# Edge weights in the scores of each quad, or in the one-hot matrices of each group

## The chip, the cores and the metric

One Trainium2 chip, one core. The metric is the device time of one execution in microseconds (us), as the median of several runs. The engines are named as in the profile: PE is TensorE (PEld its weight loads), DVE is VectorE, ACT is ScalarE, POOL is GpSimd, SP is SyncE.

## The reference

A graph layer over 6250 nodes (128 features, 8 heads of 16) and 206,250 edges, sorted by receiver. All is float32.

```python
w_ij = jax.nn.silu(edge_feats @ rad_W1 + rad_b1) @ rad_W2 + rad_b2
w_ij = w_ij + (jax.nn.silu(chi_scalar @ sph_W1 + sph_b1) @ sph_W2 + sph_b2)
w_ij = w_ij.reshape(-1, NUM_HEADS, HEAD_DIM)
q_i = (node_feats @ Wq).reshape(-1, NUM_HEADS, HEAD_DIM)[receivers]
k_j = (node_feats @ Wk).reshape(-1, NUM_HEADS, HEAD_DIM)[senders]
alpha = (q_i * w_ij * k_j).sum(axis=-1) / jnp.sqrt(jnp.float32(HEAD_DIM))
alpha = alpha * cutoffs[:, None]
v_j = (node_feats @ Wv)[senders].reshape(-1, NUM_HEADS, HEAD_DIM)
out = jax.ops.segment_sum(alpha[..., None] * v_j, receivers, num_segments=n_nodes) / AVG_NUM_NEIGHBORS
...
x = _layernorm(x + out)
```

`cutoffs` is the edge weight, one number for an edge. Each edge's message is its sender's `v`, scaled per head by `alpha`; messages are summed at the receiver.

## The kernel before

**Tiles.** 128 edges are a tile (one edge a partition), 4 tiles a quad (512 edges), 4 quads a group (2048 edges). There are 403 quads in 101 groups; the last group has three. Since edges are sorted by receiver, a quad's receivers lie in a window of 32 rows, and a group's in a window of 128.

**Before the loop** `k` and `v` of all nodes are computed and stored in HBM as `kv_tab` (1 KB a row), index tables are made, and `scale`, the edge weights of all tiles (128 x 1616), is multiplied by 1 / (4 x 16) (L463).

**Gathers.** For each tile GpSimd issues one indirect DMA (helper `gather`, L127), which fetches the 128 senders' rows of `kv_tab` into `kv`. It reads its list of row numbers from `src_i` in SBUF. `kv` has 16 buffers of a quad; the gathers of a quad are issued 14 quads ahead in program order (`AHEAD`), behind a mark of TensorE. In 26 of the quads, spread evenly, the fourth tile is fetched by SyncE with plain DMAs instead (`load_rows`, tile `wide`). The first 10 quads don't gather from the table; they gather rows of `x` (40 gathers into `msg`) and compute `k` and `v` themselves.

**One iteration of the loop** takes one slot of a group, quads in the order 0, 2, 1, 3. The order of each engine's work is written out by hand. Per quad:

- TensorE: first layers of both feature networks into `ph` (L472); `q` at the edges, `pq`, as a product with the transposed one-hot `hotT` (L481); second layers on edges into `pw` (L512, L517); and the sums of the group before, `po`, as products of `hot` and `msg` (L565, in `sum_quads`).
- ScalarE: the silu of `ph` into `act` (L502).
- VectorE: `kq = pq * kv` for the next quad (`multiply`, L526), then for this quad `kq = pw * kq` (L534), the reduction over 16 elements a head into `alpha` (L536), `alpha = alpha * scale` (L540), and `msg = v * alpha` (`messages`, L553).

`alpha` is a slice of the tile `side`, which lies in PSUM. So do `colp` and `rowwp`, the column and row numbers that the one-hots are compared with:

```python
aux = ctx.enter_context(tc.tile_pool(name="aux", bufs=1, space=PSUM))
side = aux.tile([P, QT * P], F32, name="side")
colp, rowwp = side[:, :P], side[:, P:P + 1]
alphas = side[:, 2 * P:2 * P + QT * HEADS].rearrange("p (t h) -> p t h", h=HEADS)
```

**Once a group**, beside the quads: `one_hots_T` (L218) makes `hotT` from `relb`, which a DMA brings, in slot 1; `statistics` (L623, L625, L626) adds `x` to the sums of an earlier group and takes its mean and variance, in slot 3, and every fourth group `normalize` follows it; `one_hots` (L223) makes the next group's `hot` in slot 3: 128 edges x 16 tiles x 32 window rows, 1.0 where the edge's receiver is that row. `hot` has 3 buffers.

**The last group** has one-hots over all 128 rows of its window (`wide_one_hots`), which ScalarE multiplies with `scale` (`weigh_wide`); its quads go through `scores` with `weighted=False` and leave L540 out.

Of the kernel before, what the change touches and what calls it, by code (L numbers as in the profile page):

```python
# [17 lines left out]
OP = mybir.AluOpType  # L18
AX = mybir.AxisListType
# [5 lines left out]
P = 128  # L25
N = 6250
D = 128
HEADS = 8
HD = D // HEADS
R = 32  # L30
E = 206250
GT = 16
QT = 4
# [9 lines left out]
W = 32  # L43
# [17 lines left out]
def gnn_kernel(ctx, tc, x, src, dst, weight, edges, rad_W1, rad_b1, rad_W2, rad_b2,  # L61
# [14 lines left out]
    nc = tc.nc  # L76
# [13 lines left out]
    scale = const.tile([P, NT], F32, name="scale")  # L90
# [32 lines left out]
    def quad_of(name, bufs, width=D):  # L123
        return ep.tile([P, QT, width], F32, name=name, bufs=bufs)
# [13 lines left out]
    feats_of, relb_of, act_of, kv_of, hot_of, hotT_of, x_of, q_of, msg_of = ({} for _ in range(9))  # L138
# [31 lines left out]
    def kv_parts(q, t):  # L170

        if q not in row_quads:
            return [(t, kv_of[q][:, t, :])]
        return [(slice(0, QT - 1), kv_of[q][:, :QT - 1, :]), (slice(QT - 1, QT), row_of[q])]
# [46 lines left out]
    def one_hots(g):  # L221
        hot_of[g] = gp.tile([P, GT, W], F32, name="hot", bufs=3)
        nc.vector.tensor_tensor(  # L223
            hot_of[g], rel[:, g * GT:(g + 1) * GT, None].to_broadcast([P, GT, W]),
            colp[:, None, :W].to_broadcast([P, GT, W]), op=OP.is_equal)

    def rows_from(table, at):

        return table.bitcast(U8).rearrange("n b -> (n b)")[ds(at, P * D * 4)].rearrange(
            "(p b) -> p b", p=P)  # L230
# [30 lines left out]
    with tc.tile_pool(name="nodes", bufs=1) as nodes, \  # L261
# [135 lines left out]
        def store_rel(a, b):  # L397
            for i, n in ((slice(a, min(b, NT // P)), P), (slice(NT // P, b), NT % P)):
                if i.start < i.stop:
                    t = slice(i.start * P, i.start * P + (i.stop - i.start) * n)  # L400
                    nc.sync.dma_start(rel_lin[t, :].rearrange("(n p) e -> p n e", p=n), relT[:n, i, :])
# [14 lines left out]
        n = len(chunks)  # L416
# [17 lines left out]
        for i, (k, n) in enumerate(work):  # L434
# [5 lines left out]
            if i >= len(chunks):  # L440
                kv_of[k[0]] = kvs
                a = (i - len(chunks)) * 5 // 4
# [18 lines left out]
        nc.vector.tensor_tensor(bsum, b2[:, 0:1], b2[:, 1:2], op=OP.add)  # L461
        store_rel(1, math.ceil(NT / P))
        nc.vector.tensor_scalar(scale, scale, SCALE, None, op0=OP.mult)  # L463


    with tc.tile_pool(name="ps", bufs=1, space=PSUM) as pp:
# [19 lines left out]
        def after(o, mark, reason="one signal of TensorE a quad"):  # L486
            tc.add_manual_dep(o.ins, mark.ins.name, WAIT, reason=reason)

        def behind(o, marks, k):

            if marks:
                after(o, marks[k], "a signal of TensorE behind the quad's own")

        def first_layers(q):

            return [hidden_of(q, i) for i in range(2)][-1]
# [12 lines left out]
        def weigh(q):  # L509

            pw = pp.tile([P, EQ], F32, name="pw", bufs=2)
            nc.tensor.matmul(pw, onesb, brow.rearrange("p t d -> p (t d)"), start=True, stop=False)  # L512
            pw = pw_of[q] = pw.rearrange("p (t d) -> p t d", d=D)
            marks = []
            for t in range(QT):
                for i in range(2):
                    o = nc.tensor.matmul(pw[:, t, :], act_of[q, i][:, t * P:(t + 1) * P], w2[:, i, :],  # L517
                                         start=False, stop=(t == QT - 1 and i == 1))
                    marks.append(o)
            return marks  # L520
# [7 lines left out]
                if mark is not None:  # L528
                    after(o, mark)

        def scores(q, t=slice(0, QT), marks=(), weighted=True):
            n = t.stop - t.start
            m = kq_of[q][:, t, :]
            nc.vector.tensor_tensor(m, pw_of[q][:, t, :], m, op=OP.mult)  # L534
            alpha = alphas[:, t, :]
            o = nc.vector.tensor_reduce(alpha, m.rearrange("p t (h e) -> p t h e", e=HD), AX.X, OP.add)  # L536
            behind(o, marks, 1)
            if not weighted:
                return alpha
            o = nc.vector.tensor_tensor(  # L540
                alpha, alpha,
                scale[:, q * QT + t.start:q * QT + t.stop, None].to_broadcast([P, n, HEADS]),
                op=OP.mult)
            behind(o, marks, 2)
            return alpha

        def messages(q, alpha, t=slice(0, QT), marks=()):

            if t.start == 0:
                msg_of[q] = quad_of("msg", XQ)  # L550
            for u, kv in kv_parts(q, t):
                n = u.stop - u.start
                o = nc.vector.tensor_tensor(  # L553
                    msg_of[q][:, u, :].rearrange("p t (h e) -> p t h e", e=HD),
                    kv[:, :, D:].rearrange("p t (h e) -> p t h e", e=HD),
                    alpha[:, u.start - t.start:u.stop - t.start, :, None].to_broadcast(
                        [P, n, HEADS, HD]), op=OP.mult)
                behind(o, marks, 3)
# [134 lines left out]
        marks = weigh(order[0])  # L693
        mark = marks[-1]
        for g in range(NG - 1):
            for slot, j in enumerate((0, 2, 1, 3)):
                q = g * NQ + j
                i = g * NQ + slot
                turned, past = None, mark
                if slot == 0 and g == CHECK + len(checks) + 1:  # L700
                    verdict()
                if slot == 0:
                    turned = turn_q(g + 1, pp.tile([P, EQ], F32, name="pq", bufs=2))
                if slot == 1 and 2 <= g:
                    turned = sum_group(g - 2)
                if slot == 2:
                    turned = make_q(g + 1, pp.tile([P, EQ], F32, name="pq", bufs=2))
                if 1 <= g:
                    for t in ((), (0, 1), (2,), (3,))[slot]:
                        mark = sum_quads(g - 1, t)  # L710
                first_layers(order[i + 2])
                mark = q_at_edges(order[i + 1])
                marks = weigh(order[i + 1])
                silus(order[i + 2], mark)
                if turned:
                    turned()
                if 1 <= g and slot == 3:
                    part_sums(g - 1)
                if i + AHEAD < len(order):
                    gathers(order[i + AHEAD], [past] * QT)  # L720
                multiply(order[i + 1], mark)
                messages(q, scores(q))
                if slot == 0:
                    if g + XL < NG:
                        load_x(g + XL, past)
                if slot == 2:
                    if g + 3 < NG:
                        load_feats(g + 3, past)
                    if g + 2 < NG:
                        load_rel(g + 2)  # L730
                if slot == 1:
                    one_hots_T(g + 1)
                    if g + 2 < NG:
                        pick(g + 2)
                    if 1 <= g:
                        place(g - 1)
                write_rows()
                load_rows(i)
                if slot == (3 if g < NG - 2 else 2):
                    if 2 <= g:  # L740
                        statistics(g - 2)
                if slot == 3:
                    if g + 1 < NG - 1:
                        one_hots(g + 1)
                    if CHECK <= g < CHECK + len(checks):
                        checks[g - CHECK]()
                if g == NG - 3 and slot in (0, 2):
                    wide_one_hots(order[slot // 2 - 3])
                if g == NG - 2 and slot == 0:
                    wide_one_hots(order[-1])  # L750
                    n = nc.values_load(general, min_val=0, max_val=1)
                    place(g)
                    place(NG - 1)
                if g == NG - 3 and slot in (1, 3):
                    weigh_wide(order[slot // 2 - 3])
                if g == NG - 2 and slot == 1:
                    weigh_wide(order[-1])
# [4 lines left out]
        marks = weigh(b)  # L762
# [4 lines left out]
        sd = roots(g - 3, g - 2)  # L767
        turned()
        part_sums(g - 1)
        messages(a, scores(a, weighted=False))  # L770
        multiply(b, mark)
        normalize(g - 3, g - 2, sd)
        write_rows()
# [3 lines left out]
        marks = weigh(c)  # L777
# [3 lines left out]
        for t in range(QT):  # L781
            sum_wide(a, t)
        nc.tensor.matmul(po_of[g], to_of[g][:, 1, :], tot_of[g - 1], start=False, stop=False)
        messages(b, scores(b, weighted=False))
        for t in range(QT):
            sum_wide(b, t)
        moments(g - 2, tot_of[g - 2], nc.gpsimd)
# [2 lines left out]
        sd = roots(g - 2, g)  # L790
        normalize(g - 2, g, sd)
        write_rows(2)
        alpha = scores(c, weighted=False)
        for h in halves:
            messages(c, alpha[:, h], h)
            for t in range(h.start, h.stop):
# [167 lines left out]
```

## Time and profile before

| what | value |
|---|---|
| runs | 2004.41 us median of 3 (2003.67 to 2005.16) |
| profiled execution | 2009.52 us |
| its span, first to last instruction | 2007.7 us |
| mean granted clock of TensorE | 0.920 |
| busy: TensorE / VectorE / ScalarE / GpSimd | 89% / 73% / 36% / 75% |

The profile is one execution. Rows of groups read: line, engine, operation, out<-in, shapes, count, then busy us and mean ns of one, then the idle time of that engine just before them and what ended it. Rows of the timeline read: start, length, engine, line, operation, and in brackets the idle time ahead with what ended it. Rows of waits read: engine and line that waited, for whom, us in total, how many times, the longest. Gathers are rows of L127 on POOL; what is seen there is the engine's own part, not the transfer.

### The profile page before, as it was taken

To read this page: it belongs to the slowest core of one execution; us is meant where nothing else is said; L and a number is where in the kernel's file an instruction comes from. 1 tells how busy PE (TensorE), PEld (TensorE's weight loads), DVE (VectorE), ACT (ScalarE), POOL (GpSimd) and SP (SyncE) were. 2 spreads that over 40 slices of the span, in tenths; PEclk is the share of its full clock that TensorE was granted. 3 is DMA by queue.
4 is the path that set the end of the run, shared out by engine and by line. 5 is a ranking of instruction groups with operands and counts; after the bars stand their busy time and mean duration, and the time that the engine had idled before them with its cause. 6 is when DMAs were issued, how large, how long until landed. Compare 5 with 4: busy or idle time off the path is not lost.

```text
span 2007.7 us, 48345 instructions
## 1 busy us (share of the span) xinstructions
PE 1795.3 (89%) x16014; PEld 1504.9 (75%) x16014; DVE 1469.9 (73%) x3075; ACT 716.0 (36%) x1437; POOL 1508.0 (75%) x1596
## 2 busy tenths in 40 slices
PE   9999899989798889898998898898988988988887
PEld 8788787778687777777787786777767777777776
DVE  6688687868687767776776777677767767767777
ACT  3244344424243233243242342333433323333334
POOL 7777777777777777777777777777777777777775
PEclk9899989989999899998889999989989888998898
DMA  8545555555555545545545445554455455455453
GB/s 313 160 141 153 149 148 154 153 141 154 154 143 153 152 143 152 154 143 150 156 143 151 140 141 154 155 155 140 140 154 154 143 150 157 138 142 157 139 154 89
DMA packets 146814, 304.33 MB, mean 152 GB/s; under 512 B 36941, under 2 KB 80061, under 8 KB 146557
## 3 DMA queue, kind: packets, MB, share of 16 engines
q0 software_dynamic: 75488, 205.36, 36.3%
q1 hardware_dynamic: 69568, 95.42, 14.7%
q8 instruction: 128, 2.10, 0.4%
q14 instruction: 130, 1.06, 0.2%
q10 hardware_dynamic: 1500, 0.40, 0.1%
HBM read 287.58 MB, written 13.46 MB: 150 GB/s over the span
## 4 chain that ended last, share of the span: by engine, by line
PE 25%; DMA 22%; DVE 18%; POOL 15%; issue 12%; SPq 4%; ACT 3%; DVEq 0%; POOLq 0%; ACTq 0%
DMA kv<-kv_tab,src_i 17%; POOL kv L127 14%; PE pw L517 11%; DVE kq L526 5%; PE pq L481 5%; PE ph L472 4%; DVE kq L534 4%; DVE side L536 4%; DMA relb<-rel_lin 3%; SPq L167 2%; PE po L565 2%; POOL msg L127 2%; DVE msg L553 2%; ACT y L645 1%; ACT L502 1%
## 5 line engine op out<-in xcount | busy, mean ns | idle before, releaser
L127 POOL DMA_INDIRECT kv<-kv_tab,src_i x1546 | 1467.5, 949 | 471.6 <-issue 393.2
L502 ACT ACTIVATE act<-ph,b 128x512 f32<-128x512 f32 x806 | 510.4, 684 | 1152.5 <-PE pq L481 1127.0
L517 PE MATMUL pw<-w,act 128*128 128x128 f32 x6448 | 900.8, 297 | 0.0
L517 PEld LDWEIGHTS pw<-w,act 128*128 128x128 f32 x6448 | 820.6, 206 | 102.7 <-issue 89.8
L481 PE MATMUL pq<-q,hotT 32*128 32x128 f32 x3224 | 497.1, 296 | 53.5 <-DVE hotT L218 33.6
L526 DVE TENSOR_TENSOR kq<-pq,kv 128x512 f32<-128x512 f32 (+1 forms) x403 | 273.9, 680 | 359.4 <-DMA kv<-kv_tab,src_i 203.2
L472 PE MATMUL ph<-feats,w 32*128 32x512 f32 x1612 | 497.7, 675 | 20.7 <-ACT act L502 19.8
L481 PEld LDWEIGHTS pq<-q,hotT 32*128 32x128 f32 x3224 | 417.6, 198 | 88.9 <-issue 46.3
L536 DVE TENSOR_REDUCE side<-kq 128x32 f32<-128x512 f32 x403 | 280.1, 695 | 13.9
L553 DVE TENSOR_TENSOR msg<-kv,side 128x512 f32<-128x512 f32 (+1 forms) x404 | 273.3, 677 | 13.8
L534 DVE TENSOR_TENSOR kq<-pw,kq 128x512 f32<-128x512 f32 x403 | 274.4, 681 | 0.0
L472 PEld LDWEIGHTS ph<-feats,w 32*128 32x128 f32 x1612 | 136.1, 192 | 106.3 <-issue 59.7
L512 PE MATMUL pw<-brow,onesb 3*128 3x512 bf16 x403 | 160.2, 397 | 14.4 <-DVE kq L534 14.2
L565 PE MATMUL po<-msg,hot 128*32 128x128 f32 x3200 | 158.5, 296 | 0.0
L218 DVE TENSOR_TENSOR hotT<-relb,side 128x512 f32<-128x512 bf16 x101 | 68.9, 682 | 92.5 <-DMA relb<-rel_lin 92.5
L606 PE MATMUL pq<-part,to 128*128 128x128 f32 x200 | 44.1, 304 | 72.1 <-DVE kq L526 53.8
L565 PEld LDWEIGHTS po<-msg,hot 128*32 128x32 f32 x3200 | 72.8, 113 | 39.6 <-issue 7.2
L606 PEld LDWEIGHTS pq<-part,to 128*128 128x128 f32 x200 | 31.6, 199 | 79.9 <-issue 54.6
L540 DVE TENSOR_TENSOR side<-side,scale 128x32 f32<-128x32 f32 x400 | 79.8, 199 | 13.7
L212 PE MATMUL pq<-wq,xT 128*128 128x128 f32 x200 | 45.9, 315 | 37.7 <-DVE kq L526 37.7
L212 PEld LDWEIGHTS pq<-wq,xT 128*128 128x128 f32 x200 | 34.7, 217 | 42.3 <-DVE kq L526 42.3
L223 DVE TENSOR_TENSOR hot<-rel,side 128x512 f32<-128x512 f32 x100 | 66.1, 661 | 0.0
(117 smaller groups left out, 852.3 us busy)
## 6 DMA issues: line engine op xcount, KB each, us to landing
wide<-kv_tab SPq DMA_DIRECT2D x3328, 1.0 KB
feats<-in_edges SPq DMA_DIRECT2D x101, 512.0 KB
kv<-kv_tab,src_i POOLq DMA_INDIRECT x1546
relb<-rel_lin SPq DMA_DIRECT2D x101, 128.0 KB
x<-in_x SPq DMA_DIRECT2D x101, 64.0 KB
out<-y SPq DMA_DIRECT2D x101, 64.0 KB
kv_tab<-kv SPq DMA_DIRECT2D x12, 512.0 KB
act<-in_x SPq DMA_DIRECT2D x12, 256.0 KB
```

What stands on the lines that cost most here:

```text
L127: return nc.gpsimd.indirect_dma_start(out=o, out_offset=None, in_=table, in_offset=bass.IndirectOffsetOnAxis(ap=index, axis=0))
L212: nc.tensor.matmul(pt[:n, :D], xT_of[g][:, :n], wq, start=True, stop=True)
L472: return nc.tensor.matmul(act_of[q, i], w1[r0:r0 + R, :], feats_of[g][r0:r0 + R, c0:c0 + EQ], start=True, stop=True)
L481: o = nc.tensor.matmul(pq_of[q][:, t, :], hotT_of[g][b, t * P:(t + 1) * P], q_of[g][b, :], start=True, stop=True)
L502: o = nc.scalar.activation(act, act_of[q, i], AF.Silu, bias=b1[:, i:i + 1])
L512: nc.tensor.matmul(pw, onesb, brow.rearrange("p t d -> p (t d)"), start=True, stop=False)
L517: o = nc.tensor.matmul(pw[:, t, :], act_of[q, i][:, t * P:(t + 1) * P], w2[:, i, :], start=False, stop=(t == QT - 1 and i == 1))
L526: o = nc.vector.tensor_tensor(kq_of[q][:, u, :], pq_of[q][:, u, :], kv[:, :, :D], op=OP.mult)
L534: nc.vector.tensor_tensor(m, pw_of[q][:, t, :], m, op=OP.mult)
L536: o = nc.vector.tensor_reduce(alpha, m.rearrange("p t (h e) -> p t h e", e=HD), AX.X, OP.add)
L553: o = nc.vector.tensor_tensor(msg_of[q][:, u, :].rearrange("p t (h e) -> p t h e", e=HD), kv[:, :, D:].rearrange("p t (h e) -> p t h e", e ...
L565: o = nc.tensor.matmul(po_of[g][j * W:(j + 1) * W, :], hot_of[g][:, j * QT + t, :], msg_of[g * NQ + j][:, t, :], start=(t == 0), stop=(t = ...
```

## The change

The multiplication of `alpha` by `scale` in each quad (L540) goes. In its place the one-hot matrix of a group is multiplied by the edge weights: `hot[p, t, w] *= scale[p, t]`, in place, one operation of 128 x 512 a group, right behind the operation that makes the one-hot matrix. The sums that use `hot` are then sums of weighted messages. For group 0 it stands ahead of the loop, behind L463, which makes `scale`. The last group is weighted by ScalarE as before, so there `scores` is the same as it was. On VectorE 400 operations go and 100 come; on the other engines the order of instructions is the same.

```diff
@@ one_hots
             hot_of[g], rel[:, g * GT:(g + 1) * GT, None].to_broadcast([P, GT, W]),
             colp[:, None, :W].to_broadcast([P, GT, W]), op=OP.is_equal)
+
+    def weigh_one_hots(g):
+        nc.vector.tensor_tensor(
+            hot_of[g], hot_of[g],
+            scale[:, g * GT:(g + 1) * GT, None].to_broadcast([P, GT, W]), op=OP.mult)
@@ before the loop
         nc.vector.tensor_scalar(scale, scale, SCALE, None, op0=OP.mult)
+        weigh_one_hots(0)
@@ scores
-        def scores(q, t=slice(0, QT), marks=(), weighted=True):
-            n = t.stop - t.start
+        def scores(q, t=slice(0, QT)):
             m = kq_of[q][:, t, :]
             nc.vector.tensor_tensor(m, pw_of[q][:, t, :], m, op=OP.mult)
             alpha = alphas[:, t, :]
-            o = nc.vector.tensor_reduce(alpha, m.rearrange("p t (h e) -> p t h e", e=HD), AX.X, OP.add)
-            behind(o, marks, 1)
-            if not weighted:
-                return alpha
-            o = nc.vector.tensor_tensor(
-                alpha, alpha,
-                scale[:, q * QT + t.start:q * QT + t.stop, None].to_broadcast([P, n, HEADS]),
-                op=OP.mult)
-            behind(o, marks, 2)
+            nc.vector.tensor_reduce(alpha, m.rearrange("p t (h e) -> p t h e", e=HD), AX.X, OP.add)
             return alpha
@@ the loop, slot 3
                     if g + 1 < NG - 1:
                         one_hots(g + 1)
+                        weigh_one_hots(g + 1)
```

The three calls `scores(a, weighted=False)`, with `b` and `c`, become `scores(a)` and so on.

More of the change, by code (lines that the diff above doesn't have):

```diff
@@ L769, in gnn_kernel @@
         part_sums(g - 1)
-        messages(a, scores(a, weighted=False))
+        messages(a, scores(a))
         multiply(b, mark)
@@ L783, in gnn_kernel @@
         nc.tensor.matmul(po_of[g], to_of[g][:, 1, :], tot_of[g - 1], start=False, stop=False)
-        messages(b, scores(b, weighted=False))
+        messages(b, scores(b))
         for t in range(QT):
@@ L792, in gnn_kernel @@
         write_rows(2)
-        alpha = scores(c, weighted=False)
+        alpha = scores(c)
         for h in halves:
```

## The prediction

> **What bounds the kernel now.** I read the page first, for the engine shares and the costliest groups.
>
> ```profile
> span 2007.7 us, 48345 instructions
> PE 1795.3 (89%) x16014; PEld 1504.9 (75%) x16014; DVE 1469.9 (73%) x3075; ACT 716.0 (36%) x1437; POOL 1508.0 (75%) x1596
> ...
> PE 25%; DMA 22%; DVE 18%; POOL 15%; issue 12%; SPq 4%; ACT 3%; DVEq 0%; POOLq 0%; ACTq 0%
> ...
> L127 POOL DMA_INDIRECT kv<-kv_tab,src_i x1546 | 1467.5, 949 | 471.6 <-issue 393.2
> ...
> L540 DVE TENSOR_TENSOR side<-side,scale 128x32 f32<-128x32 f32 x400 | 79.8, 199 | 13.7
> ...
> L223 DVE TENSOR_TENSOR hot<-rel,side 128x512 f32<-128x512 f32 x100 | 66.1, 661 | 0.0
> ```
>
> By the shares TensorE looks like the bound, and the chain that ended last is mixed. The row that decides is L127: 1546 gathers on GpSimd (POOL), 949 ns each, with idle time before them of 471.6 / 1546 = 0.305 us each. Is that gap a wait for somebody? The waits, and then GpSimd's timeline at the first gather from `kv_tab` and at the last ones, say no.
>
> ```profile
> POOL kv L127 <- issue: 393.2, 1289, 0.3
> ...
> 53.86 0.95 POOL L127 DMA_INDIRECT kv<-kv_tab,src_i  x1 [0.30 <-DVE brow L337]
> 55.11 0.94 POOL L127 DMA_INDIRECT kv<-kv_tab,src_i  x1 [0.30 <-issue]
> ...
> 1990.43 0.95 POOL L127 DMA_INDIRECT kv<-kv_tab,src_i  x1 [0.30 <-issue]
> 1991.69 0.94 POOL L127 DMA_INDIRECT kv<-kv_tab,src_i  x1 [0.30 <-issue]
> ```
>
> The longest of those gaps is 0.3 us, the same as all the others: it is the engine's own step from one gather to the next, whatever name stands as releaser. From 53.86 to 1991.69 lie 1545 steps, 1937.83 / 1545 = 1.2543 us each; 0.949 + 0.305 is 1.254. So GpSimd issues without a single pause for 1938 us, and whatever lengthens one gather moves all that follow. Whatever shortens work on another engine shortens nothing, unless it makes a gather shorter.
>
> That the others run behind this stream, and not ahead of it, shows in their own waits:
>
> ```profile
> DVE kq L526 <- DMA kv<-kv_tab,src_i: 203.2, 114, 5.3
> ...
> PE pq L606 <- DVE kq L526: 53.8, 30, 4.7
> ```
>
> VectorE waits 114 times for gathered data, and TensorE in its turn waits for VectorE's L526 to hand a `pq` bank back.
>
> **What in the trace lengthens a gather.** I went through GpSimd's timeline for gathers over 0.97 us and laid VectorE's timeline beside them. In the loop there are ten, and each has the same neighbour: L623, which adds `tot` and `x`, both in SBUF. Before the loop L367 is of that kind too (`rel` minus `qb`).
>
> ```profile
> 29.63 0.58 DVE L367 TENSOR_TENSOR rel<-rel,qb 128x400 f32<-128x400 f32 x1
> 30.05 0.98 POOL L127 DMA_INDIRECT msg<-in_x,src_x  x1 [0.30 <-issue]
> ...
> 33.84 0.95 POOL L127 DMA_INDIRECT msg<-in_x,src_x  x1 [0.30 <-issue]
> 33.89 0.59 DVE L367 TENSOR_TENSOR rel<-rel,qb 128x416 f32<-128x416 f32 x1
> ...
> 63.68 1.00 DVE L463 TENSOR_SCALAR scale<-scale 128x1616 f32<-128x1616 f32 x1
> 63.87 1.62 POOL L127 DMA_INDIRECT kv<-kv_tab,src_i  x1 [0.30 <-DVE kv L304]
> ...
> 259.98 0.28 DVE L623 TENSOR_TENSOR y<-tot,x 128x128 f32<-128x128 f32 x1
> 260.03 1.06 POOL L127 DMA_INDIRECT kv<-kv_tab,src_i  x1 [0.30 <-issue]
> ...
> 631.26 0.28 DVE L623 TENSOR_TENSOR y<-tot,x 128x128 f32<-128x128 f32 x1
> 631.36 1.01 POOL L127 DMA_INDIRECT kv<-kv_tab,src_i  x1 [0.30 <-DVE msg L553]
> ...
> 965.97 0.65 DVE L223 TENSOR_TENSOR hot<-rel,side 128x512 f32<-128x512 f32 x1
> 966.04 0.95 POOL L127 DMA_INDIRECT kv<-kv_tab,src_i  x1 [0.30 <-DMA kv<-kv_tab,src_i]
> ...
> 1061.34 0.95 POOL L127 DMA_INDIRECT kv<-kv_tab,src_i  x1 [0.30 <-issue]
> 1061.47 0.28 DVE L623 TENSOR_TENSOR y<-tot,x 128x128 f32<-128x128 f32 x1
> ```
>
> Read them in pairs. At 260 the addition ends at 260.26, 0.23 us into the gather, and the gather is 0.11 to 0.12 too long. At 631 it ends 0.18 in, and the gather is 0.06 to 0.07 too long. At 30 the subtraction ends 0.16 in: 0.03 too long. So the gather takes something 0.11 us after its start, and if such an operation is then running it waits until that ends: delay = end of the operation - start of the gather - 0.11. At 1061 and at 33.84 the operation starts after the gather's start and costs it nothing, though at 33.9 it runs 0.59 us. At 966 an operation of 0.65 us covers the gather's start, but one of its inputs is `side`, a PSUM tile: no delay. That the delay grows with the operation, the pair at 63.7 shows, another kind (one input, 1 us long): 64.68 - 63.87 - 0.11 = 0.70 by the formula, 0.67 seen. L623 is 0.28 us long, so its delays stay at a tenth; the new operation is longer.
>
> The Trainium skill's page "SBUF — State Buffer", section "SBUF: two separate sides", has the rule that VectorE and GpSimd share a port pair as an exclusive lock, and counts a VectorE operation with two SBUF inputs among the holders, against GpSimd operations that read SBUF; the pairs above agree.
>
> **The change part by part.** *Removed:* L540 in 400 quads. Its step on VectorE's queue is read between its own start and that of the messages, here in the last gather-bound place of the chain:
>
> ```profile
> 1961.63 2.71 DMA kv<-kv_tab,src_i
> ...
> 1966.57 0.21 DVE side L540
> 1966.80 0.69 DVE msg L553
> ```
>
> 0.23 us a quad, 400 x 0.23 = 92 us of VectorE time. One of L540's inputs is `side` in PSUM, so its going frees no gather. All of it lies behind the gather stream, but for one: the chain after the last data that it waits for (1964.34) runs through a single L540, worth -0.23 us at the end. The last three quads had none before.
>
> *Added:* one multiplication per group, 128x512 f32, `hot` by `scale`, both in SBUF, result in SBUF: 100 of them, of which 99 in the loop and one before it, right behind L463. Its length:
>
> ```profile
> L367 DVE TENSOR_TENSOR rel<-rel,qb 128x400 f32<-128x400 f32 x3 | 1.7, 576 | 0.1
> L367 DVE TENSOR_TENSOR rel<-rel,qb 128x416 f32<-128x416 f32 x1 | 0.6, 593 | 0.0
> L553 DVE TENSOR_TENSOR msg<-kv,side 128x512 f32<-128x512 f32 x376 | 258.2, 687 | 12.9
> ...
> L623 DVE TENSOR_TENSOR y<-tot,x 128x128 f32<-128x128 f32 x98 | 28.0, 285 | 0.0
> ```
>
> Two SBUF inputs go at (593 - 576) / 16 = 1.06 ns an element, so 593 + 96 x 1.06 = 695 ns; the 512-wide product with one PSUM input has 687. I take 0.69 us, 2.4 times an L623: 69 us in all. VectorE's time falls by 92 - 69 = 23 us, and that alone would be worth nothing, since the gather stream hides it.
>
> What costs is the port. With x the time from the multiplication's start to the next gather's, the delay is 0.69 - 0.11 - x where that is positive. If x is spread evenly over the 1.254 us of a step, the mean is 0.58 x 0.58 / 2 / 1.254 = 0.134 us, times 99 = 13.3 us. The bounds: never met 0, always met at worst 99 x 0.58 = 57 us. Whether x is even I tried on the trace: behind each one-hot operation of the loop
>
> ```profile
> L223 DVE TENSOR_TENSOR hot<-rel,side x100: 652/655/683, 45.5 to 1968.9; 128x512 f32<-128x512 f32 x100
> ```
>
> (99 of these rows, the first being before the loop) I laid an operation of 0.69 us, 0.035 us after its end as a dependent one, and 0.23 us earlier for the L540 gone in its quad, and took the delay from the recorded start of the next gather. That gives 13.9 us, 55 of the 99 being met. Without the 0.23 it is 16.8, with 0.46 (two quads without a stall between) 7.3, with 0.69 8.5. Even spread and projection agree; I take 13.0. The one before the loop I cost at nothing: it runs from about 64.7 to 65.4, and the next gather started at 65.80; if that comes to fall under it, 0.6.
>
> *Order and waits.* The multiplication waits for the one-hot just ahead of it on the same engine, and what stands behind it is the next quad's L526; in that one iteration of four VectorE carries 0.69 + 0.035 - 0.23 = 0.5 us more. TensorE's wait for `pq` can grow by that. But it trails the gathers as VectorE does, and the next three quads give 0.23 each back. The sums of the group read `hot` a whole group later. GpSimd's waits for a `kv` buffer were all met before, and VectorE reaches them no later relative to a delayed stream. No DMA and no queue is moved.
>
> Sum: 13.0 - 0.2 = +12.8 us. The profiled execution took 2009.52 us, 1.8 over its span and 5.1 over the median of the runs; it would become 2022.3, and the median 2004.41 + 12.8 = 2017.2.
>
> **The rivals.** First, no lock for this operation. Only an operation with one input, such as L463, would hold GpSimd back, and the L623 pairs would be chance. Then only the chain's end is left: 2004.41 - 0.2 = 2004.2, no change. For it: the delays seen are at most 0.12 us, on ten of 98 L623. Against it: they follow the formula to 0.03 us, and no L223 shows one. It decides if the gathers next to the multiplication stay at 0.95. The Trainium skill's same section warns of this trap for 2-port modes alone, and "VectorE: DVE Perf Modes", section "Why tensor_tensor can't do 2×_2P or 4×", keeps a tensor_tensor out of them; by those two the time would not change, and the pairs above speak against them.
>
> Second, VectorE is the bound after all. The chain gives it 18% of the span against 73% busy, so a quarter of its time lies on the chain; a quarter of 23 us is 6 us, and 2004.4 - 6 = 1998, faster. Against it stands the unbroken step of 1.254: it would need gathers that wait for VectorE, and there is none.
>
> Third, the phases lock. Where VectorE is stalled by a gather, its start is tied to the stream, and x could settle where most multiplications are met in the later two thirds: with x near 0.2 there, 66 x 0.4 + 33 x 0.134 = 31 us, 2035. The lump of 0.5 us in one quad of four, if TensorE had no slack, would go the same way (99 x 0.5 = 50 us).
>
> **How the numbers follow.** Two times within 0.2% (4 us) can't be told apart here. The forecast, 7 to 19 us more, gets 0.80; more than that 0.05; no lock 0.11; faster 0.04. The projections' ends, 7.3 and 16.8, less 0.2 and with some room for phases that shift, make 2010 to 2024; it leaves out the other cases and the fringe of mine. Slower by over 0.2% is 0.80 + 0.05 = 0.85, within it 0.11, faster 0.04.
>
> **What would show it.** Right: the median step of the gathers stays 1.25, but some 50 to 60 more gathers stand over 0.97 us, up to 1.53, each with the multiplication begun just ahead of it; their excess sums to the difference of the spans; VectorE's busy time is lower by 10 us or more and its waits for `kv` longer. Wrong: gathers all at 0.95 beside the multiplication (first rival), gaps on GpSimd over 0.3 us that end at VectorE (second), or an excess near 0.4 in nearly every group (third).

## The result and the profile after

| kernel | median | runs |
|---|---|---|
| before | 2004.85 us | 5 (2003.67 to 2005.20) |
| changed | 2015.06 us | 5 (2012.85 to 2015.29) |

The change makes the kernel slower: 10.2 us, ratio 1.0049 (95% interval 1.0035 to 1.0064). The profiled execution after took 2012.85 us, with TensorE at a granted clock of 0.914.

The page of the changed kernel, whose lines lie up to six places from where they were before (L228 is the new multiplication, L532 the former L526):

```profile
span 2011.1 us, 48012 instructions
PE 1814.8 (90%) x16014; PEld 1518.9 (76%) x16014; DVE 1460.0 (73%) x2775; ACT 716.0 (36%) x1437; POOL 1511.6 (75%) x1596
...
L127 POOL DMA_INDIRECT kv<-kv_tab,src_i x1546 | 1471.1, 952 | 471.3 <-issue 392.3
...
L228 DVE TENSOR_TENSOR hot<-hot,scale 128x512 f32<-128x512 f32 x100 | 69.4, 694 | 3.4
```

VectorE's busy time fell by 9.9 us, and the kernel got slower. The idle time ahead of the gathers is what it was (471.3 us), so GpSimd still waits for nobody. What grew is the gathers themselves. Here are the spread of their lengths (shortest, median and longest, in ns), and VectorE's wait for their data, which was 203.2 us in 114 places:

```profile
L127 POOL DMA_INDIRECT kv<-kv_tab,src_i x1546: 942/946/1709, 53.9 to 1995.1; - x194
...
DVE kq L532 <- DMA kv<-kv_tab,src_i: 252.3, 137, 5.2
```

The median gather is no longer than before (946 ns against 949); the mean is (952 against 949). In the timelines of GpSimd and VectorE, 46 gathers of the loop stand over 0.97 us, where before there were ten, and 43 of these have the multiplication just ahead. Two of the hundred places, and ahead of them a third (259.48) that is told of further down:

```profile
259.48 0.77 DVE L228 TENSOR_TENSOR hot<-hot,scale 128x512 f32<-128x512 f32 x1
259.52 0.95 POOL L127 DMA_INDIRECT kv<-kv_tab,src_i  x1 [0.30 <-issue]
...
1243.79 0.69 DVE L228 TENSOR_TENSOR hot<-hot,scale 128x512 f32<-128x512 f32 x1
1243.95 1.35 POOL L127 DMA_INDIRECT kv<-kv_tab,src_i  x1 [0.30 <-issue]
...
1422.30 0.69 DVE L228 TENSOR_TENSOR hot<-hot,scale 128x512 f32<-128x512 f32 x1
1422.35 1.47 POOL L127 DMA_INDIRECT kv<-kv_tab,src_i  x1 [0.30 <-DVE hot L223]
```

At 1422 the multiplication ends 0.64 us into the gather, and the gather is 1.47 - 0.95 = 0.52 too long; the formula of the prediction gives 0.53. At 1244 it ends 0.53 in: 0.40 seen, 0.42 by the formula. At 1401.10 a gather starts as the multiplication ends, and takes 0.95. Over all 100 places the excess sums to 8.1 us.

### The profile page after: what moved, and what is told of

Read it like the earlier page. It is cut to its first block, busy times and chain, and to the rows that moved or that the text cites. A ratio compares the mean times of both kernels' runs of the same rounds, so it can differ in the third digit from the quotient of the medians.

```text
span 2011.1 us, 48012 instructions
## 1 busy us (share of the span) xinstructions
PE 1814.8 (90%) x16014; PEld 1518.9 (76%) x16014; DVE 1460.0 (73%) x2775; ACT 716.0 (36%) x1437; POOL 1511.6 (75%) x1596
## 3 DMA queue, kind: packets, MB, share of 16 engines
q14 instruction: 128, 1.04, 0.2%
## 4 chain that ended last, share of the span: by engine, by line
PE 25%; DMA 25%; POOL 17%; DVE 16%; issue 11%; SPq 3%; ACT 2%; DVEq 0%; POOLq 0%; ACTq 0%
DMA kv<-kv_tab,src_i 22%; POOL kv L127 15%; PE pw L523 12%; DVE kq L532 5%; PE pq L487 5%; DVE kq L539 4%; PE ph L478 3%; DVE side L541 3%; DMA relb<-rel_lin 2%; PE po L562 2%; POOL msg L127 2%; SPq L167 2%; DVE msg L550 1%; PE pw L518 1%; DVE hot L223 1%
## 5 line engine op out<-in xcount | busy, mean ns | idle before, releaser
L127 POOL DMA_INDIRECT kv<-kv_tab,src_i x1546 | 1471.1, 952 | 471.3 <-issue 392.3
L523 PE MATMUL pw<-w,act 128*128 128x128 f32 x6448 | 912.1, 300 | 0.0
L523 PEld LDWEIGHTS pw<-w,act 128*128 128x128 f32 x6448 | 831.2, 209 | 104.8 <-issue 91.4
L487 PE MATMUL pq<-q,hotT 32*128 32x128 f32 x3224 | 501.3, 298 | 78.3 <-DVE kq L532 47.4
L532 DVE TENSOR_TENSOR kq<-pq,kv 128x512 f32<-128x512 f32 (+1 forms) x403 | 274.0, 680 | 396.2 <-DMA kv<-kv_tab,src_i 252.3
L228 DVE TENSOR_TENSOR hot<-hot,scale 128x512 f32<-128x512 f32 x100 | 69.4, 694 | 3.4
```

The source lines that it names most:

```text
L127: return nc.gpsimd.indirect_dma_start(out=o, out_offset=None, in_=table, in_offset=bass.IndirectOffsetOnAxis(ap=index, axis=0))
L487: o = nc.tensor.matmul(pq_of[q][:, t, :], hotT_of[g][b, t * P:(t + 1) * P], q_of[g][b, :], start=True, stop=True)
L532: o = nc.vector.tensor_tensor(kq_of[q][:, u, :], pq_of[q][:, u, :], kv[:, :, :D], op=OP.mult)
```

## The experiments

Three sets ran, each on one chip beside runs of the kernel before: the four named e, the same four again as f, and four named g. In e the chip granted TensorE a clock of 0.83, and before took 2605.43 us; in f and g before took 2007.16 and 2008.17. Theory: an operation of VectorE with two SBUF inputs holds the gather that starts under it, and it costs time because GpSimd's stream of gathers never pauses. Rival: the lump (0.7 us of extra work on VectorE, all of it in one quad of four) holds TensorE back. Ratios are to the kernel before on the same chip, with 95% intervals.

**e1 and f1: scale in PSUM.**

```diff
+    scalep = side[:, 3 * P:3 * P + GT]
...
+        nc.vector.tensor_copy(scalep, scale[:, g * GT:(g + 1) * GT])
         nc.vector.tensor_tensor(
             hot_of[g], hot_of[g],
-            scale[:, g * GT:(g + 1) * GT, None].to_broadcast([P, GT, W]), op=OP.mult)
+            scalep[:, :, None].to_broadcast([P, GT, W]), op=OP.mult)
```

> The change, but the 16 columns of scale that a group needs are first copied into PSUM (one small VectorE copy a group), and the multiplication reads hot from SBUF and scale from PSUM. Same amount of work on VectorE and a little more. Theory (two SBUF inputs hold the gathers): only the group's statistics hold a gather now, some ten gathers over 0.97 us, time as before, 2004 to 2006 us. Rival (the lump of 0.7 us on VectorE in one quad of four holds TensorE back): no better than the change, 2015 to 2018 us.

> The same kernel as in e1, again, since there TensorE was granted a clock of 0.83 and GpSimd paused for it. If GpSimd's stream is unbroken this time (before at about 2005 us): theory, 2004 to 2006 us, since e1 showed that the multiplication with scale in PSUM meets no gather; rival (lump on VectorE), 2015 to 2018 us. If TensorE bounds again: all within 0.4% of before.

f1: 2006.58 us against 2007.16, ratio 0.9998 (0.9989 to 1.0007). The whole cost of the change is gone, with the same lump on VectorE and a copy more. The page's rows of f1 for the gathers and the multiplication, and one place of its timeline:

```profile
L128 POOL DMA_INDIRECT kv<-kv_tab,src_i x1546 | 1465.2, 948 | 471.5 <-issue 388.3 <-DVE side L543 19.8 <-DVE kq L534 13.7
...
L230 DVE TENSOR_TENSOR hot<-hot,side 128x512 f32<-128x512 f32 x100 | 68.7, 687 | 3.5
...
805.78 0.69 DVE L230 TENSOR_TENSOR hot<-hot,side 128x512 f32<-128x512 f32 x1
805.98 0.94 POOL L128 DMA_INDIRECT kv<-kv_tab,src_i  x1 [0.31 <-issue]
```

The multiplication takes 687 ns, about as long as with both inputs in SBUF (694). At 805.98 it lies over the gather's start by 0.49 us; the formula would make the gather 0.38 too long, and it takes 0.94. Of the 99 in the loop 52 lie like this, by the formula worth 14.5 us together, and none lengthens a gather. The rival falls with this run: TensorE's wait in `pq` (L481) for VectorE's L526 was 19.8 us before and 47.4 after the change; the same wait is 48.8 in f1, and it costs nothing.

**e2 and f2: no weights.** `weigh_one_hots` of the change is never called; the weights are left out but in the last group.

```diff
-        weigh_one_hots(0)
...
                         one_hots(g + 1)
-                        weigh_one_hots(g + 1)
```

> The change without its multiplication: the edge weights are left out except in the last group, so 400 operations of VectorE are gone and none added (output not the reference's). Theory: VectorE lies behind the gather stream, so 92 us less work on it bring nothing but the 0.2 us at the end: 2004 to 2005 us, long gathers about ten. Rival (VectorE's time counts): a quarter of 92 us off, 1980 to 1990 us.

> The same kernel as in e2 (weights left out but in the last group), again. With an unbroken stream: theory, 2004 to 2005 us, 92 us of VectorE's work being worth nothing; rival (VectorE's time counts), 1980 to 1990 us. If TensorE bounds again: within 0.4% of before.

f2: 2006.83 us, ratio 1.0000 (0.9991 to 1.0009). Taking away the 400 small multiplications of before brings nothing that shows, though VectorE is busy for 1392.4 us against 1469.9; all of them were hidden.

**e3 and f3: the addition alone.** Before, with the change's multiplication put in (definition as in the change).

```diff
         nc.vector.tensor_scalar(scale, scale, SCALE, None, op0=OP.mult)
+        weigh_one_hots(0)
...
                         one_hots(g + 1)
+                        weigh_one_hots(g + 1)
```

> The kernel before with the multiplication of the change put in and the one per quad kept (weights twice, output not the reference's). Theory: the removal was worth nothing, so the added operation costs about what the change costs; only the phases to the gathers differ, since nothing comes 0.23 us earlier: the projection without that shift gave 16.8, even spread 13.3, so 2014 to 2022 us. Rival (VectorE's and TensorE's time counts): 92 us more than the change on VectorE, a quarter of it on the path, 2035 us or more.

> The same kernel as in e3 (multiplication added, the one per quad kept, weights twice), again. With an unbroken stream: theory, 2014 to 2022 us, the excess of its long gathers being the whole difference; rival, 2035 us or more. If TensorE bounds again: within 0.4% of before, whatever its long gathers sum to.

f3: 2021.71 us, 14.5 more than before, ratio 1.0068 (1.0054 to 1.0082). The gathers' row against that of f1:

```profile
L127 POOL DMA_INDIRECT kv<-kv_tab,src_i x1546 | 1480.6, 958 | 471.4 <-issue 395.5 <-DVE kq L540 15.0 <-DVE side L542 13.7
```

1480.6 - 1465.2 = 15.4 us of gathers, and 2021.71 - 2006.58 = 15.1 us of time (the two profiled executions differ by 15.1 as well). The lengthened gathers are the whole difference. 52 were lengthened by the multiplication here, 43 in the profile of the change.

**e4 and f4: four parts.**

```diff
-        nc.vector.tensor_tensor(
-            hot_of[g], hot_of[g],
-            scale[:, g * GT:(g + 1) * GT, None].to_broadcast([P, GT, W]), op=OP.mult)
+        for j in range(NQ):
+            t = slice(j * QT, (j + 1) * QT)
+            nc.vector.tensor_tensor(
+                hot_of[g][:, t, :], hot_of[g][:, t, :],
+                scale[:, g * GT + j * QT:g * GT + (j + 1) * QT, None].to_broadcast([P, QT, W]),
+                op=OP.mult)
```

> The change with its multiplication cut into four of 128x128, one for each quad of the group, one right behind the other. Theory, first form (a gather waits only for the one operation that it met): 0.285 us long each, delay 0.175 - x, mean 0.012 us, 396 of them, +5 us: 2009 to 2010 us. Second form (the next operation takes the port before the gather gets it): the four act as one of about 0.9 us, mean 0.25 us times 99, +25 us: 2025 to 2030 us. Rival (the lump on VectorE): 0.2 us longer than the lump of the change, 2015 to 2020 us, with no long gathers behind it.

> The same kernel as in e4 (multiplication in four parts of 128x128), again. e4 had only 4 of 100 groups with a gather lengthened beside it, so the first form is expected, a gather waits for no more than the one part that it met: with an unbroken stream 5 us, 2009 to 2010 us; the second form (the four act as one) 2025 us or more; rival (lump) 2015 to 2020 us. If TensorE bounds again: within 0.4% of before.

f4: 2009.73 us, ratio 1.0014 (1.0005 to 1.0023), 3.15 us over f1. The gathers' row of f4, and one place of the timeline, where the four stand in one row:

```profile
L127 POOL DMA_INDIRECT kv<-kv_tab,src_i x1546 | 1468.1, 950 | 471.5 <-issue 398.0 <-DVE side L544 16.2 <-DVE kq L535 13.1
...
457.55 0.90 DVE L230 TENSOR_TENSOR hot<-hot,scale 128x128 f32<-128x128 f32 x4
457.80 1.07 POOL L127 DMA_INDIRECT kv<-kv_tab,src_i  x1 [0.30 <-DVE hot L223]
```

Held by all four, the gather at 457.80 would be 458.45 - 457.80 - 0.11 = 0.54 too long; it is 0.12 too long. In the trace the parts start at 457.55, 457.76, 457.96 and 458.16, and the second ends at 458.04: the gather waited for that one, 0.24 us into it, and not for the two behind it, though the third had begun. So the first form holds; its size came out at about half of the 5 us expected. The same product of the same SBUF operands, with more busy time on VectorE (90.5 us for 69.4), costs a fifth of what it costs in one piece in f3.

**g1: a longer operation.** f1, in which the change holds no gather, and behind each multiplication of the loop a second one of twice the width into a spare tile.

```diff
                         weigh_one_hots(g + 1)
+                        nc.vector.tensor_tensor(
+                            junk, hot_of[g + 1][:, None].to_broadcast([P, 2, GT, W]),
+                            scale[:, None, (g + 1) * GT:(g + 2) * GT, None].to_broadcast(
+                                [P, 2, GT, W]), op=OP.mult)
```

> f1 (scale in PSUM, so that the change itself holds no gather) with one more VectorE operation a group in the loop: hot by scale, both in SBUF, into a spare tile of 128x1024, about 1.22 us long, its result unused. Theory (each gather that starts under it waits for its end): mean delay (1.22 - 0.11) squared / 2 / 1.254 = 0.49 us, times 99 = 49 us, with the phases 40 to 55: 2046 to 2062 us where before is 2007. Rival (the cost goes with the time that VectorE is busy on two SBUF inputs): 1.22 / 0.69 of what the change or f3 cost, 18 to 26 us.

g1: 2052.05 us, 43.9 over before, ratio 1.0222 (1.0206 to 1.0237). 79 of the 99 long operations lengthened a gather, by 41.7 us together, and the longest gather took 1.99 us:

```profile
1687.05 1.22 DVE L747 TENSOR_TENSOR junk<-hot,scale 128x1024 f32<-128x1024 f32 x1
1687.10 1.99 POOL L128 DMA_INDIRECT kv<-kv_tab,src_i  x1 [0.30 <-issue]
```

The formula gives 1688.27 - 1687.10 - 0.11 = 1.06, and 1.04 is seen. 1.8 times the length costs three times what f3 costs and four times what the change costs, about as the square does; by busy time it would have been 18 to 26 us.

**The set e: another bound.** The same four kernels on the chip with the lower clock:

| run | median | ratio to before, 95% interval |
|---|---|---|
| e1 scale in PSUM | 2595.48 us | 0.9964 (0.9944 to 0.9983) |
| e2 no weights | 2595.65 us | 0.9974 (0.9954 to 0.9995) |
| e3 addition alone | 2602.79 us | 0.9995 (0.9975 to 1.0014) |
| e4 four parts | 2602.46 us | 0.9992 (0.9975 to 1.0009) |

Here is the gathers' row of e3:

```profile
L127 POOL DMA_INDIRECT kv<-kv_tab,src_i x1546 | 1471.4, 952 | 996.8 <-issue 383.6 <-remote 285.9 <-PE pq L487 254.7
```

The idle time ahead of the gathers is 996.8 us, 525 more than in every profile above, and a part of it ends at TensorE (`remote` is a signal whose sender the profile doesn't name). Of the chain that ended last GpSimd has 0% there and TensorE 56%; in f3 they have 15% and 24%. 17 gathers were lengthened by the multiplication, 6.1 us together, and e3 is not measurably slower than before: the same kind of hold, with no cost that shows, because the stream has pauses and is not the bound there. Why e1 and e2 are 0.3% faster than before on that chip these runs do not settle: VectorE has no less work in e1 than before (f1, the same kernel, is busy for 1477.8 us, before for 1469.9) and 77.5 us less in e2 (f2, 1392.4), and they came out alike. What on that chip makes the kernel 30% slower is open too; the lower clock of TensorE goes with it, but its products for `pw` (L523) take only 9% longer (325 ns in e3, 299 in f3).

**g2, g3, g4: fewer gathers.** The prediction rests on the gather stream being the bound, so I tried to shorten it: more tiles of rows fetched by SyncE.

```diff
-ROW_TILES = 26
+ROW_TILES = 30
```

(34 in g3; g2 and g3 are f1 with this edit, g4 is the kernel before with it.)

> f1 with 30 instead of 26 tiles of rows fetched by SyncE instead of GpSimd, so four gathers fewer. Theory (the gather stream is the bound): 4 x 1.25 = 5 us less than before, 2002 us where before is 2007, if SyncE's queue and TensorE keep up. Rival (the others bound as much): no change, or slower by the load on SyncE's queue.

> f1 with 34 such tiles, eight gathers fewer. Theory: 10 us less than before, 1997 us where before is 2007, if SyncE's queue keeps up; rival: no change or slower.

> The kernel before with 30 such tiles. Theory: 5 us less than before, as in g2, since the 92 us of VectorE work that this kernel has more lie behind the stream. If VectorE becomes the bound as the stream gets shorter, less than g2 gains.

All three came out slower: 2117.93, 2307.43 and 2123.91 us, ratios 1.0559 (1.0537 to 1.0581), 1.1495 (1.1480 to 1.1511) and 1.0569 (1.0555 to 1.0584). One of the waits of f1 and the same of g2 point to why:

```profile
DVE hotT L219 <- DMA relb<-rel_lin: 38.6, 11, 13.3
```

```profile
DVE hotT L219 <- DMA relb<-rel_lin: 451.2, 59, 15.9
```

`relb` is loaded on SyncE's queue behind the row loads, 128 of them a tile. In f1 it comes too late 11 times, in g2 59. Of the chain that ended last SyncE's queue has 26% in g2 against 6% in f1, and the gathers now pause (531.3 us of idle time). So with four tiles more the stream no longer bounds the kernel, SyncE's queue does in good part, and what a shorter gather stream would bring could not be seen. No version beat the kernel before; f1 equals it.

## Why the prediction was right, and where it was off

**The bound.** Right. The gathers' idle time is 471.2 to 471.6 us in before, after, f1 to f4 and g1, whatever VectorE carried.

**The removal.** Costed at 0.2 us for 92 us of VectorE time; f2 shows no difference within 0.1%. Right. The forecast that VectorE's time would fall by 92 - 69 = 23 us was off, since the 92 counts whole steps and the 69 busy time alone; busy time fell by 9.9. Nothing in the sum hung on it.

**The hold.** Right in mechanism: it came with two SBUF inputs (change, f3) and went with one of them in PSUM (f1), and its size follows the formula from a length of 0.28 to 1.22 us, within 0.02 us or so. The two rules of the Trainium skill that were weighed come out as the rows had it: the port pair of "SBUF — State Buffer", section "SBUF: two separate sides", counts two SBUF inputs among the holders, and the waits that these runs show agree with it, while the port itself is in no trace; the warning of the same section, if read as naming 2-port modes alone, would have made the change free. The other way round the wait was short: a multiplication that gave way to a gather waited 0.08 us at most, and not for the gather's 0.95.

**Its sum.** The term that was mis-sized is the hold: 13.0 us forecast, 8.1 in the profile after, 10.2 between the medians. What took the profile's share from 13.0 to 8.1 can be read in three parts. First the phase, that is, where in the gathers' step the multiplications start. Put on the starts that the trace shows, with the 0.69 us of the prediction, the formula has 50 of the 99 hold a gather, not 55, for 10.6 us. The projection had shown how far the phase can move this: 7.3 to 16.8; that the forecast came as close as it did is in part luck. Second, what was not foreseen: in three places, the one at 259 among them, the multiplication started 0.03 to 0.04 us ahead of the gather, and it was the multiplication that waited (0.77 us there instead of 0.69) while the gather stayed at 0.95. By the formula these three would have been 0.54 to 0.55 each, 1.6 us of the sum. Third, the holds that were seen are 0.01 to 0.02 us shorter than the formula, 0.8 us in all: the 0.11 in it is nearer 0.13. f3, which comes 0.23 us later in its quad, was given 16.8 by the projection and had 15.1 in the profile.

**What would show it.** VectorE's waits for `kv` did grow (203.2 to 252.3 us), and its busy time fell by 9.9. Gathers over 0.97 us became 36 more, not 50 to 60, and the longest beside a multiplication took 1.47, not 1.53. The excess was to sum to the difference of the spans, and it doesn't: the lengthened gathers give 7.7 us more than before, the spans differ by 3.4. The rest is the step (from one start to the next) of the other gathers, 1.2504 us on average in this execution and 1.2533 in the one before, 4.3 us over 1500 of them. That step moves by so much from execution to execution (f2 and g1 have 1.2503, f1, f3 and f4 1.2521 to 1.2522). The one profiled execution of the change is the fastest of its five; how the 10.2 us of the medians part between holds and step stays open to some 2 us.

**The rivals.** No lock: falls with f1 beside the change. VectorE as the bound: falls with f2. Phases that lock on the worst place: not seen for the multiplication. In the set e they did pile up for another operation: in the profile of e1 the statistics' addition (L623 of before) lengthened 72 gathers with its 98 operations, 5.7 us together, against 6 gathers in f1, the same kernel with an unbroken stream; what ties them together there stays open. The lump and TensorE: TensorE's waits for L526 did grow, but f1 has the same lump, the same waits, and costs nothing.

## What to carry to other kernels

Where GpSimd issues gathers without a pause, look first at what lengthens a gather, and only then at the busy time of the others: here VectorE was busy for 10 us less and the kernel took 10 us more. A long VectorE operation with two SBUF inputs costs such a stream about the square of its length (99 of them: 8 to 15 us of holds at 0.69 us, 42 at 1.22). Put one input in PSUM, where the operation took the same time and the copy into PSUM, 0.18 us a group, was hidden; or cut it in parts: parts of 0.29 us, a quarter of the gathers' step, cost 2.8 us of holds. And ask on which chip: where the gathers paused for other reasons (e3), holds of 6.1 us showed no cost.

## What the runs showed that was not expected

Which of the two waits is settled within about 0.05 us: a multiplication that starts 0.05 us ahead of a gather can hold it (1422.30, 0.52 us); those that start 0.04 us ahead or less waited themselves, for 0.03 to 0.08 us (three in the change, as at 259.48, four in f3 and five in g1), and the gather lost nothing. A held gather waits for one operation, not for the next, even where that has already begun (f4). And one chip of the three sets ran the kernel before in 2605 us where the others took 2007 and 2008, with TensorE granted 0.82 to 0.84.
